# A state-space and expert layer: silu rebuilt from tanh tile by tile, its product on GpSimd, and four smaller edits

## The chip, the cores and the metric

One Trainium2 chip, one of its cores. A core has five engines that run their own instruction queues in order: TensorE (PE, matmuls and transposes into PSUM; PEld is its weight load), VectorE (DVE), ScalarE (ACT, activations), GpSimd (POOL, elementwise products here) and SyncE (SP, which issues the DMAs). The metric is the device time of the whole program in microseconds (us), the median of several runs. Less is better.

## The reference

The input u has 4 sequences of 2048 steps with 256 features. Two parts follow, each with a residual sum:

```
n      = layernorm(u)                                  # eps 1e-5, no affine part
x, z   = split(n @ W_in.T + b_in)                      # 512 inner channels each
dbc    = x @ W_x.T + b_x                               # 16 + 16 + 16 columns: raw delta, B, C
delta  = softplus(raw @ W_dt.T + b_dt);  A = -exp(A_log)
h      = h * exp(delta * A) + x * delta * B            # over time, 512 channels x 16 states
y      = sum_n(h * C) + x * D
u1     = u + (y * z * sigmoid(z)) @ W_out.T + b_out    # z * sigmoid(z) is silu
n      = layernorm(u1)
w      = the two largest of softmax(n @ Wg.T + bg) over 4 experts
h_e    = relu(n @ Wi.T + lowrank_e)                    # 1024 wide, rank 4 an expert
out    = u1 + sum_e w_e * (h_e @ Wo.T)
```

All numbers are float32.

## The kernel before

Time is cut into 16 chunks of 512 steps. Channels lie on the 128 partitions, so a chunk has four channel tiles (ND = 4) of 128 x 512, and each of them has 16 states: 64 scans of 128 x 512 a chunk, 1024 in all. "State i" below is the i-th of these scans.

The loop over the states (lines after `for i in range(M + 4)`) gives each state: `decay` (ACT, exp of delta times A into a PSUM tile dA of a pool of three banks, two states ahead), `enter` (POOL, the product dBx of x times delta with B for two states at once, four states ahead, three buffers), `scan` (DVE, one instruction over 512 steps, in place in PSUM, or into SBUF as hS for one state in four), `read` (the product with C: DVE's hC, or for that one in four POOL's hP), `keep` (ACT copies the last column as the carry) and `sum_y` (PE transposes the product and adds it up in the PSUM tile y). B and C come from DRAM by broadcast DMAs on SP, some groups of four states ahead.

Everything else is a list of steps that is filled in between the states: `front` (LayerNorm statistics on DVE, its reciprocal root on POOL in `rstd`, normalising on ACT, transposes, the projections `p_in`, `p_dbc`, `p_dt`, softplus over all four tiles in one activation), the gate (`p_in` for z, `a_in` with the bias, and `silu`, one activation over 128 x 2048), `tail` (out projection and residual), and `ffn` (routing, then the inner layer by half rows of 512). Front and gate run for the chunk to come, the inner layer lags by up to two chunks. A `Pacer` writes the order out by hand: it carries planned times for each engine, places a step where its own plan lets it start in time (BEGIN, END, MARGIN are its limits), counts three PSUM banks for all such steps (`takes`, `gives`), and forces steps that others are about to need (`force`: the silu before a chunk's y is closed, softplus and the delta-x products before the next chunk's first product). It plans one order for each engine; the chip then runs these orders.

In the inner layer, half row k (NK = 8 a chunk) takes one bank. Before the change `p_base` opens it with two matmuls by Wi, `p_low` adds the low-rank part of the second expert's slot, a first relu reads it, `p_low` of the next k adds the first slot's part, a second relu reads it, and `p_hT` transposes both relus together; `p_down` multiplies by Wo.

ACT holds one set of function tables at a time; a load stands before softplus and silu, and another before the exp that follows. In the first chunk the name `xdts` for the products of delta and x is taken over by the next chunk's, so the forcing at state 27, which is meant for chunk 0's last product, asks for chunk 1's.

Of the kernel before, what the change touches and what calls it, by code (L numbers as in the profile page):

```python
# [13 lines left out]
P = 128  # L14
# [30 lines left out]
class Pacer:  # L45
# [6 lines left out]

    BEGIN = {"pe": 0.7, "act": 0.6, "pool": 0.5, "sp": 0.0}
    END = {"pe": 2.2, "act": 1.5, "pool": 2.5, "sp": 99.0}
# [114 lines left out]
def ssm_moe_layer_kernel(  # L169
# [115 lines left out]
    nc.gpsimd.memset(lowm, 0.0)  # L285

    carry = const.tile([P, ND, N], F32, tag="carry", name="carry")

# [4 lines left out]
    pacer = Pacer(BANKS)  # L293
    st = {}

# [28 lines left out]
    def layernorm_T(src, dst, name, then=None):  # L324

        q = {}

        def stats(j):
            if j == 0:
                q["mv"] = small.tile([P, NJ, 2], F32, tag=f"mv{name[0]}", name=f"mv_{name}")  # L330
            x = small.tile([P, 6], F32, tag="st", name=f"st_{name}_{j}")
            dve.bn_stats(x, src()[:, j, :])
            dve.bn_aggr(q["mv"][:, j, :], x)

        def rstd():

            ve = small.tile([P, NJ], F32, tag="ve", name=f"ve_{name}")
# [25 lines left out]

        steps = [Step("dve", 0.54, lambda j=j: stats(j)) for j in range(NJ)]
        steps += [Step("pool", 1.95, rstd)]
# [26 lines left out]
    def front(c, norm, taken=()):  # L392
# [13 lines left out]
        def hold(k):  # L406
            if k not in s:
                s[k] = chunk.tile([P, ND, TC], F32, tag=k, name=f"{k}_{c}")
            return s[k]

        def a_in(dst, m, mw):
            act.activation(hold(dst)[:, m, :], q["in", mw], AF.Identity, bias=b_in_sb[:, mw : mw + 1])

# [37 lines left out]
        def xdt(m):  # L451
            pool.tensor_tensor(hold("xdt")[:, m, :], s["delta"][:, m, :], s["xT"][:, m, :], ALU.mult)

        def silu():
            act.activation(s["g"], s["g"], AF.Silu)

# [23 lines left out]
        for m in range(ND):  # L480
            gate.append(Step("pe", 1.75, lambda m=m: p_in(ND + m), after=[ln], takes=1))
            gate.append(Step("act", 0.57, lambda m=m: a_in("g", m, ND + m), gives=1))
        gate.append(Step("act", 4.4, silu))
        return steps, gate, dbc, xdts

    def open_y(c, d):
# [5 lines left out]
        def scale():  # L492
            q["xd"] = work.tile([P, TC], F32, tag="xd", name=f"xd_{c}_{d}", bufs=1)
            act.activation(q["xd"], s["xT"][:, d, :], AF.Copy, scale=d_sb[:, d : d + 1])

# [62 lines left out]
    def ffn(c):  # L558
# [102 lines left out]
        def p_base(k):  # L661
            j, half = divmod(k, 2)
            pm = q["z", k] = mm_tile(f"pz_{c}_{k}")
# [74 lines left out]
        z1s, hs, copies = [], [], []  # L738
        bases = [Step("pe", 1.75, lambda k=k: p_base(k), after=[last], takes=1) for k in range(NK)]
        steps.append(bases[0])  # L740
# [119 lines left out]
    def begin(c):  # L860
# [13 lines left out]
        if c + 1 < NCHUNK:  # L874
            norm = norms.pop(c + 1, None) or front_norm(c + 1)
            f, g, *deadline[c + 1] = front(c + 1, norm[NJ if c else 0 :], [g[-3]])
            g[0].after += gate_after
            silus[c + 1] = g[-1]
            if not c:
# [16 lines left out]
    act.activation(spare, mhalf[:, 0:1], AF.Softplus)  # L896
    f, g, dbc, xdts = front(0, front_norm(0))
    pacer.add(f)
    pacer.force(f[2 * NJ])
    join_x()  # L900
    pacer.force(dbc)
    silus[0] = g[-1]
# [5 lines left out]
    pacer.force(xdts[0])  # L908

# [3 lines left out]
    for i in range(0, AHEAD_B, NN):  # L913
        pacer.force(xdts[states[i][2]])
        X[i] = X[i + 1] = pacer.run("pool", 2.32, lambda: enter(i))
# [8 lines left out]
    for i in range(M + 4):  # L924
# [109 lines left out]
```

## Time and profile before

| what | value |
|---|---|
| median of 3 runs | 2129.7 us (2126.46 to 2132.01) |
| profiled execution | 2129.43 us, span 2127.7 us |
| granted TensorE clock, mean | 0.929 |
| busy: PE, DVE, POOL, ACT | 88%, 87%, 80%, 68% of the span |
| first scan starts, last scan ends | 31.6, 2014.8 us |
| scans on DVE | 1024, 1.21 to 1.28 us each |
| dBx products on POOL | 512, 2.363 us each |
| table loads on ACT | 64, 1.283 us each |

A group's row in the profile has the line, the engine, the operation, what it writes and reads, the count, then the busy time in us and the mean length of one in ns, then the idle time of the engine just before them and what ended most of it. A row in order of time has the start and the length in us, and in brackets the idle time before it and who ended it. A row of waits has who waited for whom, the sum in us, how often, and the longest. Instructions of one engine overlap by some 0.03 to 0.1 us, so a busy sum is a little over the time it fills, and where steps are added up the distance from start to start is used. All steps pass through one helper, so their line is L30, and groups are told apart by their tiles.

### The profile page before, as it was taken

Reading aid. Unit: us, or ns where it says so; the run is one execution under the profiler, and the core shown is the slowest. Engines: PE = TensorE matmul, PEld = TensorE weight load, DVE = VectorE, ACT = ScalarE, POOL = GpSimd, SP = SyncE. Lnnn points to the kernel's source line nnn. Section 1 sums busy time; section 2 is a strip of 40 time slices with the busy share of each in tenths; the row PEclk is TensorE's granted clock in tenths of the full one; section 3 lists DMA queues with packets and bytes.
Section 4 is the critical chain, followed back from the end, with each engine's and each line's share of the span. In section 5 each row is a group of like instructions: output and inputs, shape, how many; then the busy total and the mean of one; then the engine's idle time right before and its main releaser. Section 6 shows DMA issues by size and latency. Waiting matters only on the chain.

```text
span 2127.7 us, 28591 instructions
## 1 busy us (share of the span) xinstructions
PE 1873.9 (88%) x9504; PEld 1284.0 (60%) x9504; DVE 1855.8 (87%) x2423; ACT 1441.7 (68%) x2898; POOL 1709.4 (80%) x1084
## 2 busy tenths in 40 slices
PE   7768788998889989899899988989899998989978
PEld 4445555665566665657666565766657575666655
DVE  4899898999989989999989998999989999999810
ACT  5857667667676667676767777676677867766522
POOL 5898888989878878888888888888888888878600
PEclk9859799998999999999999999999999999989989
DMA  7454344445444443434435454444535444444200
GB/s 218 144 165 152 127 150 149 149 147 161 151 139 151 149 140 138 169 130 149 163 130 164 140 167 132 147 152 139 169 130 173 136 141 149 138 149 140 98 10 10
DMA packets 106132, 300.70 MB, mean 141 GB/s; under 512 B 12864, under 2 KB 39104, under 8 KB 105984
## 3 DMA queue, kind: packets, MB, share of 16 engines
q1 hardware_dynamic: 105984, 298.88, 42.8%
q8 instruction: 74, 1.21, 0.2%
q14 instruction: 74, 0.61, 0.1%
HBM read 289.41 MB, written 9.44 MB: 140 GB/s over the span
## 4 chain that ended last, share of the span: by engine, by line
PE 25%; DVE 20%; ACT 12%; issue 5%; POOL 1%; DVEq 0%; POOLq 0%; ACTq 0%
DVE dA L30 9%; PE pz L30 9%; PE y L30 5%; PE pf L30 5%; ACT dA L30 5%; DVE hC L30 4%; DVE hS L30 4%; PE phT L30 3%; ACT L30 2%; ACT h L30 1%; PE pin L30 1%; ACT delta L30 1%; ACT g L30 1%; DVE u L30 1%; DVE plg L30 1%
## 5 line engine op out<-in xcount | busy, mean ns | idle before, releaser
L30 POOL TENSOR_TENSOR dBx<-xdt,B 128x1024 f32<-128x1024 f32 x512 | 1207.8, 2363 | 187.5 <-DVE dA L30 157.3
L30 ACT ACTIVATE dA<-delta,a_sb 128x512 f32<-128x512 f32 x1024 | 706.8, 693 | 143.0 <-DVE hC L30 66.8
L30 DVE TENSOR_TENSOR_SCAN dA<-dA,carry,dBx 128x512 f32<-128x512 f32 x576 | 726.4, 1279 | 62.6 <-ACT dA L30 51.0
L30 PE MATMUL y<-ident,hC 128*128 128x128 f32 x3072 | 490.7, 291 | 36.6 <-DVE hC L30 36.5
L30 DVE TENSOR_TENSOR hC<-dA,C 128x512 f32<-128x512 f32 x768 | 514.1, 670 | 0.2 <-issue 0.2
L30 PEld LDWEIGHTS y<-ident,hC 128*128 128x128 f32 x3072 | 386.1, 150 | 181.3 <-issue 73.6
L30 POOL TENSOR_TENSOR hP<-hS,C 128x512 f32<-128x512 f32 x256 | 326.6, 1276 | 5.1 <-issue 4.1
L30 PE MATMUL pz<-wi_sb,x2T 128*128 128x512 f32 x512 | 271.7, 657 | 25.2 <-ACT hT L30 15.4
L30 DVE TENSOR_TENSOR_SCAN dA<-dA,dBx 128x512 f32<-128x512 f32 x192 | 231.2, 1220 | 35.3 <-ACT dA L30 30.5
L30 DVE TENSOR_TENSOR_SCAN hS<-dA,carry,dBx 128x512 f32<-128x512 f32 x192 | 244.1, 1271 | 18.6 <-ACT carry L30 10.6
L30 PE MATMUL pf<-wo_sb,hT 128*128 128x256 f32 x1024 | 243.4, 383 | 11.6 <-ACT hT L30 9.4
L30 PE MATMUL pin<-xnT,w_in_sb 128*128 128x512 f32 x512 | 245.9, 612 | 5.5 <-ACT g L30 3.6
L30 ACT COPY carry<-dA 128x1 f32<-128x1 f32 x576 | 90.1, 157 | 208.5 <-DVE hC L30 206.5
L30 ACT ACTIVATE h<-pz,topv 128x512 f32<-128x512 f32 x256 | 165.4, 680 | 74.1 <-PE pz L30 73.4
L30 PEld LDWEIGHTS pf<-wo_sb,hT 128*128 128x128 f32 x1024 | 186.5, 190 | 41.6 <-ACT hT L30 14.4
L30 PEld LDWEIGHTS y<-ident,hP 128*128 128x128 f32 x1024 | 128.3, 148 | 96.3 <-issue 56.7
L30 PE MATMUL y<-ident,hP 128*128 128x128 f32 x1024 | 167.1, 288 | 18.7 <-POOL hP L30 18.7
L30 PEld LDWEIGHTS pz<-wi_sb,x2T 128*128 128x128 f32 x512 | 95.2, 207 | 124.9 <-issue 76.2
L30 PE MATMUL pz<-bm_sb,lowT 16*128 16x512 f32 x512 | 167.9, 660 | 0.0
L30 PE MATMUL phT<-ident,h 128*128 128x128 f32 x1024 | 139.7, 281 | 21.3 <-ACT h L30 16.8
L30 PEld LDWEIGHTS pin<-xnT,w_in_sb 128*128 128x128 f32 x512 | 92.3, 197 | 93.1 <-issue 75.2
L30 PEld LDWEIGHTS phT<-ident,h 128*128 128x128 f32 x1024 | 120.8, 145 | 44.2 <-ACT h L30 19.5
(94 smaller groups left out, 1784.8 us busy)
## 6 DMA issues: line engine op xcount, KB each, us to landing
B<-bc SPq DMA_DIRECT2D x256, 512.0 KB, 3.7
C<-bc SPq DMA_DIRECT2D x256, 512.0 KB, 3.7
ua<-in_u_dram SPq DMA_DIRECT2D x16, 512.0 KB, 5.5
u<-in_u_dram SPq DMA_DIRECT2D x16, 512.0 KB, 4.4
out_dram<-u SPq DMA_DIRECT2D x16, 512.0 KB, 4.8
w_in_sb<-in_w_inT_dram SPq DMA_DIRECT2D x2, 512.0 KB, 4.7
wi_sb<-in_wiT_dram SPq DMA_DIRECT2D x1, 1024.0 KB, 6.7
wo_sb<-in_woT_dram SPq DMA_DIRECT2D x1, 1024.0 KB, 10.4
```

What stands on the lines that cost most here:

```text
L30: return self._tc.keep_in_program_order(f(*args, **kwargs))
```

## The change

Silu is computed as (1 + tanh(z/2)) * z/2. `a_half` writes z/2 in place of z (the bias halved once at the start in `bh_sb`, on POOL, and a scale of 0.5); `tanh` is two activations for each channel tile, tanh and the addition of 1, into a tile th with two buffers; `silu` is a product on POOL for each tile. The tile m waits for the product of two tiles before. Closing a y forces only its own tile's product.

The low-rank part of slot 1 opens the inner layer's bank (`start` moves from `p_base` to `p_low`), and `p_base` comes behind it; the bank is taken there, and the base of the next half row no longer starts ahead.

In LayerNorm the addition of eps and the sign of the mean go from POOL to DVE, as two operations on the four columns of mv behind the last statistics; POOL keeps the power and one product.

`first_xdts` keeps chunk 0's products apart, so the forcing at state 27 asks for these.

x is held in half-chunk tiles with three buffers, in place of one tile a chunk with two. The planner lets POOL's steps begin up to 1.0 in place of 0.5 ahead of DVE's plan, and its costs follow the new steps. The built program has 32 table loads in place of 64.

```
-    BEGIN = {"pe": 0.7, "act": 0.6, "pool": 0.5, "sp": 0.0}
+    BEGIN = {"pe": 0.7, "act": 0.6, "pool": 1.0, "sp": 0.0}
...
+    bh_sb = const.tile([P, ND], F32, tag="bh_sb", name="bh_sb")
+    nc.gpsimd.tensor_scalar_mul(bh_sb, b_in_sb[:, ND:], 0.5)
...
             dve.bn_aggr(q["mv"][:, j, :], x)
+            if j == NJ - 1:
+                q["nm"], q["ve"] = q["mv"][:, :, 0], q["mv"][:, :, 1]
+                dve.tensor_scalar_mul(q["nm"], q["nm"], -1.0)
+                dve.tensor_scalar(q["ve"], q["ve"], EPS, None, ALU.add)
...
-            pool.tensor_scalar_add(ve, q["mv"][:, :, 1], EPS)
-            pool.tensor_tensor(q["rstd"], ve, mhalf, ALU.pow)
-            pool.tensor_tensor(ve, q["mv"][:, :, 0], q["rstd"], ALU.mult)
-            pool.tensor_scalar_mul(q["nmr"], ve, -1.0)
+            pool.tensor_tensor(q["rstd"], q["ve"], mhalf, ALU.pow)
+            pool.tensor_tensor(q["nmr"], q["nm"], q["rstd"], ALU.mult)
...
+        def x_of(m):
+            k = "xT", m // ND2
+            if k not in s:
+                s[k] = chunk.tile([P, ND2, TC], F32, tag="xT", name=f"xT_{c}_{m // ND2}", bufs=3)
+            return s[k][:, m % ND2, :]
...
-        def silu():
-            act.activation(s["g"], s["g"], AF.Silu)
+        def a_half(m):
+            mw = ND + m
+            act.activation(hold("g")[:, m, :], q["in", mw], AF.Identity, bias=bh_sb[:, m : m + 1], scale=0.5)
+
+        def tanh(m):
+            q["th", m] = work.tile([P, TC], F32, tag="th", name=f"th_{c}_{m}")
+            act.activation(q["th", m], s["g"][:, m, :], AF.Tanh)
+            act.activation(q["th", m], q["th", m], AF.Copy, bias=1.0)
+
+        def silu(m):
+            g = s["g"][:, m, :]
+            pool.tensor_tensor(g, q["th", m], g, ALU.mult)
...
-            gate.append(Step("act", 0.57, lambda m=m: a_in("g", m, ND + m), gives=1))
-        gate.append(Step("act", 4.4, silu))
+            gate.append(Step("act", 0.57, lambda m=m: a_half(m), gives=1))
+            gate.append(Step("act", 1.02, lambda m=m: tanh(m)))
+            gate[-1].after = gate[-2:-1] + halves[-2:-1]
+            gate.append(Step("pool", 1.23, lambda m=m: silu(m)))
+            halves.append(gate[-1])
...
         def p_base(k):
-                    start=(m == 0), stop=False, skip_group_check=True,
+                    start=False, stop=True, skip_group_check=True,
...
         def p_low(k):
+                    if slot:
+                        q["z", x] = mm_tile(f"pz_{c}_{x}")
...
-                        rhs=bm_sb[r, half * HF : (half + 1) * HF], start=False, stop=True,
+                        rhs=bm_sb[r, half * HF : (half + 1) * HF], start=bool(slot), stop=not slot,
...
-                "pe", 1.06 if 0 < k < NK else 1.05, lambda k=k: p_low(k), after=bases[k : k + 1] + z1s[-1:]
+                "pe", 1.06 if 0 < k < NK else 1.05, lambda k=k: p_low(k), after=[last] + z1s[-1:], takes=int(k < NK)
...
-                z1s.append(Step("act", 0.57, lambda k=k: a_relu(k, 1), after=[low]))
-                steps.append(z1s[-1])
-            steps += bases[k + 1 : k + 2]
+                bases.append(Step("pe", 1.75, lambda k=k: p_base(k), after=[low]))
+                z1s.append(Step("act", 0.57, lambda k=k: a_relu(k, 1), after=bases[-1:]))
+                steps += [bases[-1], z1s[-1]]
...
-                pacer.force(silus[c])
-                steps[0].after = [pacer.run("act", 0.5, copy, [Y[i - 3]]), silus[c]]
+                pacer.force(silus[c][d])
+                steps[0].after = [pacer.run("act", 0.5, copy, [Y[i - 3]]), silus[c][d]]
...
             if i == PER // NH - AHEAD_B - 1:
-                pacer.force(xdts[-1])
+                pacer.force(first_xdts[-1])
```

More of the change, by code (lines that the diff above doesn't have):

```diff
@@ L293, in ssm_moe_layer_kernel @@
     pacer = Pacer(BANKS)
-    st = {}
+    st, halves = {}, []
     wc_sb = const.tile([P, KM, NX + R], F32, tag="wc_sb", name="wc_sb")
@@ L333, in stats @@
             dve.bn_aggr(q["mv"][:, j, :], x)
+            if j == NJ - 1:
+                q["nm"], q["ve"] = q["mv"][:, :, 0], q["mv"][:, :, 1]
+                dve.tensor_scalar_mul(q["nm"], q["nm"], -1.0)
+                dve.tensor_scalar(q["ve"], q["ve"], EPS, None, ALU.add)
         def rstd():
-            ve = small.tile([P, NJ], F32, tag="ve", name=f"ve_{name}")
             q["rstd"] = small.tile([P, NJ], F32, tag="rstd", name=f"rstd_{name}")
             q["nmr"] = small.tile([P, NJ], F32, tag="nmr", name=f"nmr_{name}")
-            pool.tensor_scalar_add(ve, q["mv"][:, :, 1], EPS)
-            pool.tensor_tensor(q["rstd"], ve, mhalf, ALU.pow)
-            pool.tensor_tensor(ve, q["mv"][:, :, 0], q["rstd"], ALU.mult)
-            pool.tensor_scalar_mul(q["nmr"], ve, -1.0)
+            pool.tensor_tensor(q["rstd"], q["ve"], mhalf, ALU.pow)
+            pool.tensor_tensor(q["nmr"], q["nm"], q["rstd"], ALU.mult)
         def norm(j):
@@ L364, in layernorm_T @@
         steps = [Step("dve", 0.54, lambda j=j: stats(j)) for j in range(NJ)]
-        steps += [Step("pool", 1.95, rstd)]
+        steps += [Step("pool", 1.35, rstd)]
         steps += [Step("act", 0.5, lambda j=j: norm(j), locks=j == 0) for j in range(NJ)]
@@ L409, in hold @@
             return s[k]
+        def x_of(m):
[3 more added lines that the diff above has]
+            return s[k][:, m % ND2, :]
+        s["x"] = x_of
         def a_in(dst, m, mw):
-            act.activation(hold(dst)[:, m, :], q["in", mw], AF.Identity, bias=b_in_sb[:, mw : mw + 1])
+            act.activation(x_of(m) if dst == "xT" else hold(dst)[:, m, :], q["in", mw], AF.Identity, bias=b_in_sb[:, mw : mw + 1])
         def p_dbc():
@@ L451, in xdt @@
         def xdt(m):
-            pool.tensor_tensor(hold("xdt")[:, m, :], s["delta"][:, m, :], s["xT"][:, m, :], ALU.mult)
-        def silu():
-            act.activation(s["g"], s["g"], AF.Silu)
+            pool.tensor_tensor(hold("xdt")[:, m, :], s["delta"][:, m, :], x_of(m), ALU.mult)
+        def a_half(m):
[8 more added lines that the diff above has]
+            pool.tensor_tensor(g, q["th", m], g, ALU.mult)
         steps = list(norm)
@@ L493, in scale @@
             q["xd"] = work.tile([P, TC], F32, tag="xd", name=f"xd_{c}_{d}", bufs=1)
-            act.activation(q["xd"], s["xT"][:, d, :], AF.Copy, scale=d_sb[:, d : d + 1])
+            act.activation(q["xd"], s["x"](d), AF.Copy, scale=d_sb[:, d : d + 1])
         def turn():
@@ L662, in p_base @@
             j, half = divmod(k, 2)
-            pm = q["z", k] = mm_tile(f"pz_{c}_{k}")
+            pm = q["z", k]
             for m in range(KM):
@@ L738, in ffn @@
         z1s, hs, copies = [], [], []
-        bases = [Step("pe", 1.75, lambda k=k: p_base(k), after=[last], takes=1) for k in range(NK)]
-        steps.append(bases[0])
+        bases = []
         for k in range(NK + 1):
             low = Step(
-                "pe", 1.06 if 0 < k < NK else 1.05, lambda k=k: p_low(k), after=bases[k : k + 1] + z1s[-1:]
+                "pe", 1.06 if 0 < k < NK else 1.05, lambda k=k: p_low(k), after=[last] + z1s[-1:], takes=int(k < NK)
             )
@@ L875, in begin @@
             norm = norms.pop(c + 1, None) or front_norm(c + 1)
-            f, g, *deadline[c + 1] = front(c + 1, norm[NJ if c else 0 :], [g[-3]])
+            f, g, *deadline[c + 1] = front(c + 1, norm[NJ if c else 0 :], [g[-4]])
             g[0].after += gate_after
-            silus[c + 1] = g[-1]
+            silus[c + 1] = g[3::4]
             if not c:
@@ L896, in ssm_moe_layer_kernel @@
     act.activation(spare, mhalf[:, 0:1], AF.Softplus)
-    f, g, dbc, xdts = front(0, front_norm(0))
+    f, g, dbc, first_xdts = front(0, front_norm(0))
     pacer.add(f)
@@ L901, in ssm_moe_layer_kernel @@
     pacer.force(dbc)
-    silus[0] = g[-1]
+    silus[0] = g[3::4]
     loaded = next(x for x in f if x.engine == "sp")
@@ L907, in ssm_moe_layer_kernel @@
         load_bc(i, 1)
-    pacer.force(xdts[0])
+    pacer.force(first_xdts[0])
     act.activation(a_sb, a_sb, AF.Exp)
@@ L913, in ssm_moe_layer_kernel @@
     for i in range(0, AHEAD_B, NN):
-        pacer.force(xdts[states[i][2]])
+        pacer.force(first_xdts[states[i][2]])
         X[i] = X[i + 1] = pacer.run("pool", 2.32, lambda: enter(i))
```

## The prediction

> **What bounds the kernel now.** I read the page first, then the stretches before and after the last scan, then the groups of VectorE and ScalarE, then the order of time around one silu and around the last chunk.
>
> ```profile
> span 2127.7 us, 28591 instructions
> PE 1873.9 (88%) x9504; PEld 1284.0 (60%) x9504; DVE 1855.8 (87%) x2423; ACT 1441.7 (68%) x2898; POOL 1709.4 (80%) x1084
> ```
>
> No engine is full over the whole span, so it has to be cut. The busy time by stretch (us of PE, PEld, DVE, ACT, POOL, then granted clock, DMA share, GB/s); the first scan starts at 31.6, the last ends at 2014.8:
>
> ```profile
> 31.60:2014.80 1983.20, 1759.39 (x9040) 1211.82 (x9040) 1839.58 (x2374) 1396.83 (x2824) 1699.75 (x1056) 0.93 0.45 148
> 2014.80:2071.90 57.10, 44.26 (x208) 31.91 (x206) 10.06 (x31) 14.27 (x27) 3.11 (x10) 0.86 0.03 10
> 2071.90:2127.70 55.80, 49.68 (x196) 28.45 (x196) 1.70 (x4) 15.51 (x25) 0.00 (x0) 0.96 0.03 10
> ```
>
> For 1983 us the 1024 scans run, and DVE is busy in 93% of it; its true idle time there, gap by gap, is 134 us, and 116 of them end with ACT. After that 113 us belong to PE. What ends DVE's idle time, and what the largest of it is:
>
> ```profile
> DVE dA L30 <- ACT dA L30: 81.5, 129, 6.1
> ...
> DVE hS L30 <- ACT carry L30: 21.0, 10, 6.5
> ...
> L30 ACT ACT_TABLE_LOAD x64 | 82.1, 1283 | 1.8 <-PEq L1021 0.7
> ...
> L30 ACT ACTIVATE g<-g 128x2048 f32<-128x2048 f32 x16 | 30.6, 1912 | 0.2
> ...
> 102.89 1.28 ACT L30 ACT_TABLE_LOAD   x1
> 104.19 1.91 ACT L30 ACTIVATE g<-g 128x2048 f32<-128x2048 f32 x1
> ...
> 106.16 1.28 ACT L30 ACT_TABLE_LOAD   x1
> 107.46 0.69 ACT L30 ACTIVATE dA<-delta,a_sb 128x512 f32<-128x512 f32 x1
> ...
> 108.18 2.35 DVE L30 TENSOR_TENSOR_SCAN dA<-dA,dBx 128x512 f32<-128x512 f32 x2 [2.20 <-ACT dA L30]
> ```
>
> The reader is to see one silu: load, 2048 columns, load back, and only then the decay that the next scan needs. Three dA banks let ACT run two states ahead, about 3.5 us of DVE work; 4.4 us between two decays overrun it by 2.2.
>
> **The change, part by part** (orders are those of the two built programs, durations are rows of this execution).
>
> Silu. 32 of 64 table loads and 16 long activations go. DVE's idle time before the scan behind each was 2.3, 2.2, 2.4, 2.8, 0, 1.4, 2.3, 1.6, 2.2, 1.8, 2.1, 1.6, 2.2, 1.8, 2.1, 2.1: 30.6 us. All of it goes: -30.6 (ends -31 and -25). ACT's own time hardly changes: 2 x 1.295 + 1.82 = 4.4 us a chunk from start to start against four times two activations of 128x512. Tanh is in no row; hT<-phT takes 585 ns and dA 693, so a dependent pair is 1.15 to 1.35, four are 4.6 to 5.4. The Trainium skill, "ScalarE: Activation LUTs", section What ACT_TABLE_LOAD costs, puts a switch at 1283 ns plus a drain of about 1380; by it 32 switches would free 85 us of ACT, by the row (next instruction 1.295 behind) 41. The trace decides, and ACT's total time isn't the bound.
>
> What comes in their place. Between two decays the new order has 61 places with 1.5 to 4 us of other ACT work, where the old has 27; 26 of these lay in the loop with whole rows, and none was followed by an idle DVE. Places with 0.25 to 1.25 us go from 598 to 622, and cost 0.1 each before (59.6 us in 598). So tanh costs 2.4 plus 34 x 0.15 = 7; ends 0 and 34 x 0.5 = 17 + 2.4. I take 7, near the rows that stalled nothing.
>
> Softplus. 15 stand in the loop and cost 23.9 us, 13 unforced ones 0.65 each, up to 2.3. In the new order 14 stand alone; 14 x 0.65 = 9, at the worst like the silus 14 x 2 = 28. The wrong delta: state 27 of chunk 0 forced chunk 1's last delta x, which put its softplus at state 29 with 6.15 us of ACT work and an idle time of 6.07. Now chunk 1's front is held until its own deadline: LayerNorm, transposes and dbc (3.52 us of ACT) at state 52, xT, four deltas and softplus (7.88) at 56. The rows are 6.07 for 6.15 and 6.45 for 6.73; I take 9 for both, 6 to 14. Together 18 against 23.9: -6 (-9 to +18). With it the two bc writes of 32 KB and the next ua load move on SP's queue from behind the B loads of states 16 to 20 to those of state 48; write and B load land in 3.2 + 3.7 us, the first product that reads them is issued at state 60, 8 x 1.9 us on, so they stay covered. If they were late, the first scan of chunk 1 would wait by the difference.
>
> LayerNorm. POOL loses two small operations in each of 32 (228 and 242 ns), DVE gains two. On DVE the last aggregation is now waited for: 0.21 where the next started 0.10 behind, and two operations at 0.09 (m's step): 0.3 x 31 in the loop = +9 (6 if only the steps count, 12 if the first costs its full 0.18). DVE is the engine in want there, so it is charged in full; in the tail POOL's shorter chain pays it back.
>
> POOL gets 64 products at the rate of xdt, 1.225 from start to start: 4.9 us a chunk, less 1.2 for LayerNorm. A chunk's POOL work goes from 106.4 to some 110 us of 124. dBx waits for DVE 157 us in all today, so there is room; bursts of eight states reach 19 us where 18.2 passed without a stall. +3 (0 to 8). What is queued behind a product on POOL is dBx, four states ahead; DVE's gate multiply, which now waits for it, stands at least six states later. A tanh waits for the product two tiles before; if POOL were late, a decay behind it on ACT would be late with it, and a PSUM bank held.
>
> The half bias. The new product stands ahead of the first rstd on POOL and waits for b_in_sb, issued at 8.33, landing 1.8 later; rstd started at 7.47. The normalised tiles come 2.5 us later, but the transposes waited for PE until 12.7 anyway: +0.5.
>
> Banks. With the low-rank part first, PE's sequence per half row is low, base, phT; relu 1 (0.68) is covered by phT (0.96). In steady state nothing changes. What changes is how far the inner layer has come when the scans end:
>
> ```profile
> 2053.63 0.69 DVE L30 TENSOR_TENSOR u<-u,po 128x512 f32<-128x512 f32 x1 [2.71 <-PE po L30]
> ...
> 2059.19 2.80 PE L30 MATMUL pt_f<-ident,xn_f 128*128 128x128 f32 x8 [5.59 <-ACT xn_f L30]
> ...
> 2071.89 1.06 PE L30 MATMUL plT<-ident,lowm 128*64 128x128 f32 x4 [6.05 <-POOL lowm L30]
> ...
> 2086.22 1.04 PE L30 MATMUL phT<-ident,h 128*128 128x128 f32 x8
> ```
>
> Behind the last y the old order holds 3 base pairs of chunk 14, 9 low, 40 phT and 24 pf matmuls up to plT; the new one 7, 13, 64 and 32. That is 4 x 1.82 + 4 x 0.53 + 3 x 0.96 + 3.65 + one wait of 0.68 = 16.6 us more PE work after the scans. But the two chains in which PE stood idle (5.59 and 6.05) now have 4 us and 3.5 us of chunk 14 beside them: -7.5 to -8. Net +8 (5 to 12).
>
> The sum: -30.6 + 7 - 6 + 9 + 3 + 0.5 + 8 = -9. The profiled execution took 2129.43 (span 2127.7), like the median of 2129.7; I predict 2120. All good ends together give -28, all bad ones +45.
>
> **Where a row fails.** The two new DVE operations read and write SBUF with one source. No row shows such a multiply or add beside a POOL product: the one on a_sb ran while POOL was idle.
>
> ```profile
> L30 DVE RECIPROCAL sm<-sm 128x4 f32<-128x4 f32 x16 | 2.9, 178 | 0.6
> ...
> L30 DVE TENSOR_SCALAR a_sb<-a_sb 128x64 f32<-128x64 f32 x1 | 0.2, 195 | 15.0 <-ACT a_sb L30 15.0
> ```
>
> The nearest is the reciprocal, SBUF to SBUF, four columns: 10 of 16 ran beside a POOL product, all started 0.035 behind their forerunner and took 177 to 179 ns. So the sum has no wait. The far end: each waits for the product in flight. The Trainium skill, "SBUF — State Buffer", section Who interferes with whom, says that a one-source multiply between SBUF operands may use two ports and then is locked out for the whole of a GpSimd instruction; the reciprocal isn't in its list.
>
> **The rivals.**
>
> 1. DVE waits for POOL (slower). At the end of the last aggregation POOL was inside an instruction in 20 of 32 cases, with 0.6 us left on the mean of all. If the first operation waits: 31 x 0.6 = 19. If the second then waits for the next product, 20 x 1.3 to 2.4 = 26 to 47 more. On -9 that is +10 to +57: 2139 to 2186, and 2152 if the second waits 1.3 in half of the 20. It decides as soon as the mean wait of a LayerNorm is over 0.5 us. For it: POOL is busy in 86% of the loop. Against: the reciprocals.
>
> 2. The stalls are only cut in pieces (same). Each of 64 tanh pairs overruns its place by 0.3 us: 19 in place of 7, softplus right after the scans' y tiles close costs 1.2 in place of 0.65 (+8). Sum +11: 2131. For it: 14 softplus now stand where the silus stood. Against: places of 1.5 to 2 us that stalled nothing.
>
> 3. The inner layer isn't later on chip than before, since PE catches up in DVE's new idle time; then the +8 goes and it ends at 2112. Against: the order is fixed, and PE has 11% idle at a clock of 0.93.
>
> **How the numbers follow.** The forecast has 0.50 with its own range 2105 to 2135, rival 1 has 0.25, rival 2 0.18, rival 3 0.07. This kernel's runs tell 0.3% (6.4 us) from nothing: faster is under 2123, slower over 2136. Of the forecast 0.36 lies under, 0.12 between, 0.02 over; rival 3 is faster; rival 2 gives 0.13 same, 0.03 faster, 0.02 slower; rival 1 gives 0.23 slower and 0.02 same. Faster 0.46, same 0.27, slower 0.27. 2100 takes in all good ends; 2165 leaves out the upper half of rival 1's second wait: 2100 to 2165.
>
> **What would show it.** 32 table loads; the scans end some 17 us earlier, at 1997, and the part behind them is 8 longer. No stall over 1 us stands outside softplus. The new operation on mv_a takes some 0.1 to 0.2 us and starts at once; a mean wait of 0.5 us or more, with POOL in front, is rival 1. If DVE's idle time ended by ACT isn't near 86 us, the silu term failed; if POOL ends more than 15, the POOL term.

## The result and the profile after

| | before | after |
|---|---|---|
| median of 20 runs each | 2130.45 us (2126.46 to 2132.31) | 2134.02 us (2118.42 to 2144.47) |
| ratio after / before, 95% interval | | 1.0016 (0.9999 to 1.0033) |
| span of the profiled execution | 2127.7 | 2137.4 |
| first scan starts, last scan ends | 31.6, 2014.8 | 32.2, 2019.1 |
| from the last scan to the end | 112.9 | 118.3 |
| DVE idle between first and last scan, summed over gaps of more than 0.06 us | 133.7 | 106.7 |

No difference that can be measured: 2120 was forecast, 14 us less than the median. The profiled execution of after took 2139.22, 5 above its median, so its span overstates the change by that much. The head of the page of after:

```profile
span 2137.4 us, 28813 instructions
PE 1897.9 (89%) x9504; PEld 1301.8 (61%) x9504; DVE 1886.1 (88%) x2487; ACT 1448.1 (68%) x2978; POOL 1767.7 (83%) x1085
```

DVE is busy for 30.3 us more (1855.8 before) and has 64 more instructions. The same cut by stretch (us, busy time of PE, PEld, DVE, ACT, POOL, granted clock, DMA share, GB/s) shows where:

```profile
32.20:2019.10 1986.90, 1766.79 (x8974) 1221.28 (x8973) 1869.54 (x2434) 1395.60 (x2894) 1758.87 (x1060) 0.91 0.44 147
2019.10:2077.00 57.90, 56.53 (x258) 37.14 (x257) 7.45 (x20) 20.03 (x33) 1.22 (x2) 0.96 0.00 1
2077.00:2137.40 60.40, 52.78 (x212) 31.12 (x211) 4.50 (x18) 17.36 (x30) 1.40 (x6) 0.96 0.05 18
```

In the first stretch DVE's busy time rose by 29.9 (1839.58 before) while its idle time fell by 27.0: what the rest of the change gave there was spent, and the loop is 3.7 longer. Behind the scans PE is busy in 109.3 of 118.3 us, where it was busy in 93.9 of 112.9. DVE's longest waits and the groups of instructions that the change added:

```profile
DVE dA L30 <- ACT dA L30: 59.1, 125, 3.0
...
DVE hS L30 <- ACT carry L30: 16.9, 4, 9.9
```

```profile
L30 ACT ACT_TABLE_LOAD x32 | 41.1, 1283 | 1.3 <-PEq L1051 0.7
L30 ACT ACTIVATE th<-th 128x512 f32<-128x512 f32 x64 | 40.4, 631 | 2.0
L30 ACT ACTIVATE th<-g 128x512 f32<-128x512 f32 x64 | 39.8, 622 | 1.0
...
L30 DVE TENSOR_SCALAR mv_a<-mv_a 128x4 f32<-128x4 f32 x32 | 27.5, 902 | 0.6
L30 DVE TENSOR_SCALAR mv_f<-mv_f 128x4 f32<-128x4 f32 x32 | 4.7, 191 | 0.6
```

The wait for the decay is down from 81.5 to 59.1. The last two rows are the two small operations of LayerNorm: 902 ns on the mean for four columns in the LayerNorm of u (mv_a), 191 in the one of u1 (mv_f). The view of the one tile gives least, median and longest:

```profile
L30 DVE TENSOR_SCALAR mv_a<-mv_a x32: 155/602/4362, 6.9 to 1705.4; 128x4 f32<-128x4 f32 x32
```

And this is the longest of them in order of time:

```profile
1699.46 2.49 POOL L30 TENSOR_TENSOR xdt<-delta,xT 128x512 f32<-128x512 f32 x2
...
1700.92 0.18 DVE L30 BATCH_NORM_AGGREGATE mv_a<-st_a 128x2 f32<-128x6 f32 x1
1701.14 4.43 DVE L30 TENSOR_SCALAR mv_a<-mv_a 128x4 f32<-128x4 f32 x2
...
1701.91 2.35 POOL L30 TENSOR_TENSOR dBx<-xdt,B 128x1024 f32<-128x1024 f32 x1
...
1704.21 1.26 POOL L30 TENSOR_TENSOR xdt<-delta,xT 128x512 f32<-128x512 f32 x1
1705.48 1.27 DVE L30 TENSOR_TENSOR_SCAN hS<-dA,carry,dBx 128x512 f32<-128x512 f32 x1
```

The multiply starts at 1701.14, inside a product on POOL, and ends at 1705.50, when POOL's third product in a row ends at 1705.47. No semaphore is waited for: the wait lies inside the instruction, so the profile counts it as busy time, and a list of waits doesn't show it. The others are of the same kind: 19 of the 64 took over 0.22 us, and each of them started inside a POOL instruction and ended 24 to 32 ns behind the end of one. For 14 it was the product in flight. Four, each the second of its pair, started in the last 0.06 us of the product that the first had waited for, and waited for the whole of the next; the one shown waited through three. Without waits the 64 operations would take some 0.16 each (155 to 171 ns in the other 45), 10 us; they take 32.2 as the rows count them, and 35.0 summed one by one, since a row counts the overlap of a pair once. So some 25 us of DVE's time are waits for POOL.

### The profile page after: what moved, and what is told of

It is laid out like the page before. It is cut to its first block, busy times and chain, and to the rows that moved or that the text cites. A ratio compares the mean times of both kernels' runs of the same rounds, so it can differ in the third digit from the quotient of the medians.

```text
span 2137.4 us, 28813 instructions
## 1 busy us (share of the span) xinstructions
PE 1897.9 (89%) x9504; PEld 1301.8 (61%) x9504; DVE 1886.1 (88%) x2487; ACT 1448.1 (68%) x2978; POOL 1767.7 (83%) x1085
## 5 line engine op out<-in xcount | busy, mean ns | idle before, releaser
L30 PE MATMUL y<-ident,hC 128*128 128x128 f32 x3072 | 501.0, 296 | 39.7 <-DVE hC L30 39.4
L30 PEld LDWEIGHTS y<-ident,hC 128*128 128x128 f32 x3072 | 395.7, 153 | 187.7 <-issue 72.0
L30 PE MATMUL pz<-wi_sb,x2T 128*128 128x512 f32 x512 | 263.2, 639 | 0.0
L30 ACT ACTIVATE h<-pz,topv 128x512 f32<-128x512 f32 x256 | 173.3, 680 | 132.3 <-PE pz L30 131.5
L30 DVE TENSOR_TENSOR_SCAN dA<-dA,dBx 128x512 f32<-128x512 f32 x192 | 231.7, 1220 | 20.5 <-ACT dA L30 14.9
L30 PE MATMUL y<-ident,hP 128*128 128x128 f32 x1024 | 174.3, 297 | 50.0 <-POOL hP L30 50.0
L30 PE MATMUL pz<-bm_sb,lowT 16*128 16x512 f32 x512 | 175.0, 670 | 26.6 <-ACT delta L30 8.3
L30 PEld LDWEIGHTS pz<-wi_sb,x2T 128*128 128x128 f32 x512 | 93.7, 204 | 102.1 <-issue 102.1
L30 PE MATMUL phT<-ident,h 128*128 128x128 f32 x1024 | 135.3, 275 | 7.9 <-ACT h L30 7.0
```

Of the source, the lines that this page charges most:

```text
L30: return self._tc.keep_in_program_order(f(*args, **kwargs))
```

## Experiments: the LayerNorm operations

The kernel before was run beside each of these, at medians of 2129.6 to 2131.1, and the ratios are to those runs.

Theory 1: the multiplies are locked out by POOL's instructions, and this is what ate silu's gain. Rivals: the waits are taken up by idle time elsewhere, or the gain of silu was never there.

**The same operations as reductions.** Everything else of after stays, the orders of PE, ACT, POOL and SP too but for four fills of constants at the start. eps is added by summing the variance and a third column that holds it.

```
-                dve.tensor_scalar_mul(q["nm"], q["nm"], -1.0)
-                dve.tensor_scalar(q["ve"], q["ve"], EPS, None, ALU.add)
+                dve.tensor_reduce(q["nm"], q["mv"][:, :, 0:1], AX.X, ALU.add, negate=True)
+                dve.tensor_reduce(q["ve"], q["mv"][:, :, 1:3], AX.X, ALU.add)
```

> The changed kernel with LayerNorm's two small DVE operations written as reductions (the sign by a reduction over one column with negation, eps by a sum over the variance and a third column that holds eps); every engine's order stays. Theory lock (an SBUF-to-SBUF multiply or add on DVE waits for the POOL product in flight): the two groups on DVE fall from 32.2 us to about 5.5, no single one is over 0.25 us, and some 20 to 27 us of the span go: 2107 to 2114, and the spread of its runs shrinks. Theory dispatch (DVE loses the time to the wait for the last aggregation and to having two more operations, whatever their kind): the time stays at 2134 within 5.

Measured: 2102.31 (2100.02 to 2104.57), ratio to before 0.9868 (0.9855 to 0.9881), 31.7 us under after. The groups of this run:

```profile
L30 DVE TENSOR_REDUCE nm_a<-mva 128x4 f32<-128x4 f32 x16 | 2.5, 157 | 0.6
...
L30 DVE TENSOR_REDUCE ve_a<-mva 128x4 f32<-128x8 f32 x16 | 2.4, 151 | 0.0
```

37 of the 64 reductions ran within a POOL instruction, none took over 159 ns. The scans end at 1980.2 (after 2019.1), the part behind them is 118.0 (118.3). The time is some 5 under theory lock's range: by the two profiles DVE's busy time in the loop fell by 26.1, as the theory has it, and its idle time by 13.0 as well. Why the idle time fell isn't shown. The Trainium skill, "SBUF — State Buffer", section Who interferes with whom, says that a reduction has no two-port mode on this chip and so never contends with GpSimd: these rows agree. The rows of mv_a agree with what the same section says of a `tensor_scalar`, that it can enter the two-port modes and then contends.

**The LayerNorm part undone.** eps and sign go back to POOL as four small operations, DVE loses its two; the orders of PE, ACT and SP are those of after.

```
-                dve.tensor_scalar_mul(q["nm"], q["nm"], -1.0)
-                dve.tensor_scalar(q["ve"], q["ve"], EPS, None, ALU.add)
...
+            pool.tensor_scalar_add(ve, q["mv"][:, :, 1], EPS)
+            pool.tensor_tensor(q["rstd"], ve, mhalf, ALU.pow)
+            pool.tensor_tensor(ve, q["mv"][:, :, 0], q["rstd"], ALU.mult)
+            pool.tensor_scalar_mul(q["nmr"], ve, -1.0)
```

> The kernel after with its LayerNorm part alone undone: eps and sign go back to POOL, DVE loses the two operations; the orders of PE, ACT and SP are the ones of after. Theory 1 (the two DVE multiplies are locked out by POOL's products, and this costs the whole program its full length): what after spends on them is 32.2 us, and POOL gets 0.47 us back in each of 32 LayerNorms at 90% busy, so 2134 - 32 + (0 to 8) = 2102 to 2110, and the scans end some 25 us earlier than after's 2019.1. Rival (the waits are taken up by idle time elsewhere, as in the kernel before plus the LayerNorm part alone, and what made the reductions faster was another thing): 2125 to 2137, the scans end at 2010 to 2020, and DVE's idle time in the loop grows from 106.7 to 125 or more.

Measured: 2105.70 (2105.24 to 2107.47), ratio 0.9883 (0.9871 to 0.9896): theory 1. Its stretch of scans:

```profile
32.20:1986.20 1954.00, 1743.97 (x8976) 1210.75 (x8977) 1837.67 (x2374) 1396.27 (x2895) 1773.10 (x1120) 0.92 0.45 150
```

The row begins at after's 32.2; by its own first scan, at 32.0, the loop is 32.7 us shorter than after's. DVE's busy time is 31.9 lower, and its idle time is the same, 106.7. In this order the waits and the operations' own time cost their full length. With the two operations on DVE as reductions the kernel is 3.4 us faster than with them on POOL (2102.31 against 2105.70); the intervals overlap.

**The operations doubled.** Two more multiplies, by 1.0, behind the two.

```
                 dve.tensor_scalar(q["ve"], q["ve"], EPS, None, ALU.add)
+                dve.tensor_scalar_mul(q["nm"], q["nm"], 1.0)
+                dve.tensor_scalar_mul(q["ve"], q["ve"], 1.0)
```

> The kernel after with two further multiplies by 1.0 in each LayerNorm, on the same columns and straight behind the two that are there: 64 more operations on DVE, the result unchanged, all orders else as in after. Theory 1 (a LayerNorm pays for the lock once: the first operation waits for the product in flight, and behind it POOL is mostly idle, because its next operation waits for these): 64 x 0.1 to 0.17, 6 to 11 us more, 2140 to 2145. Theory 2 (each operation waits for itself, at the mean of 0.5 us that the 64 of after took): 32 us more, 2166, and to 2190 if POOL's products get in between.

Measured: 2151.19 (2147.77 to 2155.48), 17.2 more, between the two:

```profile
L30 DVE TENSOR_SCALAR mv_a<-mv_a 128x4 f32<-128x4 f32 x64 | 52.6, 877 | 0.6
L30 DVE TENSOR_SCALAR mv_f<-mv_f 128x4 f32<-128x4 f32 x64 | 8.4, 186 | 0.6
```

The mean of one hardly changes (902 to 877, 191 to 186), so the second pair pays about as much as the first: by place in the row of four they took 22.0, 14.1, 24.6 and 7.3 us in all. The scans ended 17.7 later while these rows grew by 28.8, since DVE's idle time fell from 106.7 to 97.3.

**The LayerNorm part alone on the kernel before**, once with multiplies as in the change, once with reductions. The first has before's orders on PE, ACT and SP:

```
-            pool.tensor_scalar_add(ve, q["mv"][:, :, 1], EPS)
-            pool.tensor_tensor(q["rstd"], ve, mhalf, ALU.pow)
-            pool.tensor_tensor(ve, q["mv"][:, :, 0], q["rstd"], ALU.mult)
-            pool.tensor_scalar_mul(q["nmr"], ve, -1.0)
+            pool.tensor_tensor(q["rstd"], q["ve"], mhalf, ALU.pow)
+            pool.tensor_tensor(q["nmr"], q["nm"], q["rstd"], ALU.mult)
```

> The kernel before with the LayerNorm part of the change alone; the order of PE, ACT and SP is that of before, and POOL has two small operations less in each of 32. Theory lock: the new DVE operations take 20 to 35 us in all, single ones 2 to 4 us, and the time is 15 to 25 us over before: 2145 to 2155. Theory dispatch: 64 operations at 0.1 and a wait of 0.1 each: 6 to 9 us over before, 2136 to 2139.

> The kernel before with the LayerNorm part alone, its two DVE operations written as reductions, which in the changed kernel took 151 to 157 ns each. With multiplies the same edit gave 2127.3, and the multiplies took 26.4 us of DVE there. Theory 1 (the lock costs its full length wherever DVE is in want): 26.4 - 9.8 = 16.6 us less, 2111, the range 2108 to 2116. Theory 2 (in the order of before, idle time behind ACT took up most of the waits, 133.7 us of it fell to 106.1): a third of that comes back, 2120 to 2126, and DVE's idle time in the loop returns to 118 to 130.

Measured: with multiplies, against both expectations of a loss, 2127.33 (2123.07 to 2133.18), ratio 0.9987 (0.9977 to 0.9998), though they took 26.4 us:

```profile
L30 DVE TENSOR_SCALAR mv_a<-mv_a 128x4 f32<-128x4 f32 x32 | 20.5, 684 | 0.6
L30 DVE TENSOR_SCALAR mv_f<-mv_f 128x4 f32<-128x4 f32 x32 | 5.9, 229 | 0.6
```

With reductions 2121.86 (2119.07 to 2123.85), ratio 0.9960 (0.9948 to 0.9973): 5.5 us less, where the operations became 16.6 us shorter. So the lock is there too, but in before's order two thirds of it vanish in idle time: DVE's fell from 133.7 to 106.1 with multiplies and stands at 116.1 with reductions. Theory 2 of the second expectation holds in its time; the idle time is a little under its 118. And without the lock the move to DVE is no loss: with reductions it is 0.4% faster than before. That the cover is the time behind silus and decays, in which ACT catches up while DVE waits for POOL, is read from which gaps shrank (the wait of dA for ACT went from 81.5 to 66.9 and back to 72.6), not tested by itself.

## Experiments: silu, the banks and the part behind the scans

**The silu part alone** on the kernel before (tanh, the product on POOL, x in half chunks; the lines are those of the change's diff), and **the bank part alone**, and **both**. The core of the second is

```
-        bases = [Step("pe", 1.75, lambda k=k: p_base(k), after=[last], takes=1) for k in range(NK)]
-        steps.append(bases[0])
+        bases = []
...
+                bases.append(Step("pe", 1.75, lambda k=k: p_base(k), after=[low]))
+                z1s.append(Step("act", 0.57, lambda k=k: a_relu(k, 1), after=bases[-1:]))
```

> The kernel before with silu by tanh, its product on POOL and x in half chunks, and nothing else. The prediction's terms: 30.6 us of stalls go, 7 come back, 3 for POOL. Its order has 118 us of PE matmul work behind the last y where before has 86 (at the steps of the last chunk of before), so the part behind the scans grows by 32 less what fills the two chains, 12 at most. Theory that the silu part pays its gain back behind the scans: scans end 15 to 25 us earlier than 2015, the rest is 20 to 30 longer, time 2125 to 2140. Theory that the tanh pairs stall the scans anew: scans end at 2005 or later and the time is over 2140.

> The kernel before with the low-rank part opening the inner layer's banks and nothing else. Behind the last y its order has 77 us of PE work where before has 86; the silus and softplus stay. Theory banks (a bank that is held for a shorter time lets the inner layer run further ahead): the part behind the scans is 6 to 10 us shorter, the scans end where they did, 2120 to 2124. Theory that the chain low, base, relu, low is longer and stalls ACT and through it the scans: no gain or a loss, 2130 to 2140.

> The kernel before with the silu part (2153.6 alone) and the low-rank part first in the banks (2134.7 alone) together. PE work in the built order behind the last y: 118.0 us with silu alone, 99.3 with both. Theory (the banks shorten the part behind the scans by what they move ahead of the last y, as 9.5 us of order gave 10.5 us on the chip): the rest goes from 143.5 to 123 to 126. In the loop the banks alone cost 15 us through relus that wait for PE ahead of decays on ACT (143.9 us of such waits against 73.4): if that is their nature, 2153.6 - 19 + 15 = 2150; if it was that order alone, 2135. A relu wait sum near 144 with the scans ending over 2022 is the first, near 131 with 2010 to 2015 the second.

| kernel | median | ratio (95%) | scans end | the rest (last scan to end) | PE work behind the last y in the built order | relus waiting for PE |
|---|---|---|---|---|---|---|
| before | 2130.45 | | 2014.8 | 112.9 | 86.2 | 73.4 |
| silu alone | 2153.62 | 1.0105 (1.0090 to 1.0121) | 2010.6 | 143.5 | 118.0 | 80.5 |
| banks alone | 2134.73 | 1.0020 (1.0012 to 1.0029) | 2029.8 | 102.4 | 76.7 | 143.9 |
| silu and banks | 2138.29 | 1.0032 (1.0018 to 1.0047) | 2016.3 | 124.6 | 99.3 | 133.3 |
| after | 2134.02 | 1.0016 (0.9999 to 1.0033) | 2019.1 | 118.3 | 102.1 | 131.5 |

(The sixth column counts matmuls of each kind by the time that each takes from start to start in before.) Against the expectations: silu alone has the longer rest of its first theory, but its time (over 2140) and its scans' end (after 2005) are those of the second, in which the tanh pairs stall the scans. Tanh pairs aren't what is seen, though. The longest of DVE's waits, the last number of this row, is 25.3 us in chunk 0,

```profile
DVE dA L30 <- ACT dA L30: 91.7, 133, 25.3
```

where the old forcing at state 27, which these kernels keep, puts all of chunk 1's front between two decays. Chunk 0 idles 30.9 us there, 13.2 before (small gaps counted). Banks alone fall in the second theory's 2130 to 2140. Both together lie between the two times named, with the rest (124.6) as expected and the relu waits and the scans' end near the second.

Three things follow. The rest goes with the lag of the inner layer that the planner builds: silu alone makes it 31.8 us of work and 30.6 us of time longer, and the banks take back 18.7 of work and 18.9 of time. So on the kernel before it is under the silu part that the planner lets the inner layer fall back, and the banks pull it forward, where the prediction had put the whole lag under the banks.

Second, the banks aren't free in the loop: alone they let the scans end 15.0 us later. The waits of ACT's relus for PE, before and with the banks alone:

```profile
ACT h L30 <- PE pz L30: 73.4, 67, 4.9
```

```profile
ACT h L30 <- PE pz L30: 143.9, 122, 5.9
```

One of them in order of time (banks alone), with DVE's scan behind it:

```profile
380.14 3.78 PE L30 MATMUL pz<-wi_sb,x2T 128*128 128x512 f32 x4
...
384.02 0.69 ACT L30 ACTIVATE h<-pz,topv 128x512 f32<-128x512 f32 x1 [3.60 <-PE pz L30]
...
384.65 0.70 ACT L30 ACTIVATE dA<-delta,a_sb 128x512 f32<-128x512 f32 x1
...
385.44 1.29 DVE L30 TENSOR_TENSOR_SCAN dA<-dA,carry,dBx 128x512 f32<-128x512 f32 x1 [2.96 <-issue]
```

The relu waits for its bank's base matmuls, which no longer start a half row ahead; the decay queued behind it on ACT is late, and the scan with it. Beside silu the same waits cost less: 133.3 us of them, but the scans end only 5.7 us later than with silu alone.

Third, silu and banks by themselves gain nothing in the loop: DVE's idle time is 132.5 with both, 133.7 before. The kernel without the LayerNorm part (2105.70) differs from this one (2138.29) only in `first_xdts`, in POOL's earlier begin (1.0 in place of 0.5) and in the planner's cost of a LayerNorm's POOL step (1.35 in place of 1.95), and is 32.6 us faster. The old forcing alone is worth 13.0 of it, as measured below beside reductions. By difference some 20 us hang on the planner's two numbers, which no run changes by themselves. The prediction prices the order that they helped to make, but has no term for them.

**The bank part undone in after**, with reductions in place of the locked multiplies; the base matmuls open the bank again:

```
+        bases = [Step("pe", 1.75, lambda k=k: p_base(k), after=[last], takes=1) for k in range(NK)]
+        steps.append(bases[0])
```

> The kernel after with the two LayerNorm operations as reductions (2102.3 alone), and the bank part undone: the base matmuls open the bank again, one half row ahead. In the built order 88.0 us of PE work stand behind the last y, 102.1 with the bank part. Theory 1 (the built order's lag sets the part behind the scans, and in this kernel the bank part makes it longer; it also makes relus wait for PE ahead of decays): the rest goes from 118 to 104, ACT's relu waits for PE from 118.5 to some 75 us, the loop is 0 to 15 us shorter, 2073 to 2088. Theory 2 (the bank part shortens what stands behind the scans, as it did by 10.5 us alone and by 19 us beside the silu part): the rest grows by 10 to 19, 2112 to 2121.

Measured: 2110.14 (2098.99 to 2113.88), ratio 0.9901 (0.9880 to 0.9922), 7.8 more than with the banks (2102.31); the intervals just touch. The relu waits fell to 67.7 and the rest to 111.7 (profiled at 2102.49), which is theory 1 for both, though the rest by 6 in place of 14. So in this order it is the bank part that makes the lag: 14.1 of the 15.9 us of PE work by which after's order exceeds before's. But the time missed theory 1's 2073 to 2088: the loop became 9.3 longer (1957.2 against 1947.9), where 0 to 15 less was expected. The planner makes another order when a bank is held longer, and some chunks stall more: chunk 4 lost 14.9 us in idle time in place of 4.8, chunk 0 22.5 in place of 19.1 (here and below small gaps are counted too). So the single price of the bank part has no fixed sign: it cost 4 us on before, gave 15 beside silu and 8 here, and costs 19 in the pair of kernels at the end of the next part. It depends on the order that the planner makes around it.

## Experiments: the first chunk

In after, chunk 0 has two stalls, the two largest of the loop, where the front of chunk 1 is held until its deadlines at states 52 and 56. The second in the rows of ACT and of DVE:

```profile
133.13 0.69 ACT L30 ACTIVATE xT<-pin,b_in_sb 128x512 f32<-128x512 f32 x1 [0.80 <-PE pin L30]
135.28 0.69 ACT L30 ACTIVATE xT<-pin,b_in_sb 128x512 f32<-128x512 f32 x1 [1.47 <-PE pin L30]
136.33 2.59 ACT L30 ACTIVATE delta<-pdt,b_dt_sb 128x512 f32<-128x512 f32 x4 [0.36 <-PE pdt L30]
138.94 1.28 ACT L30 ACT_TABLE_LOAD   x1
140.23 1.91 ACT L30 ACTIVATE delta<-delta 128x2048 f32<-128x2048 f32 x1
...
144.29 1.22 DVE L30 TENSOR_TENSOR_SCAN hS<-dA,dBx 128x512 f32<-128x512 f32 x1 [9.88 <-ACT carry L30]
```

ACT not only has 7.88 us of work in a row here, it also waits inside the burst for PE's projections, 2.6 us in the three rows shown. The first stall, of 5.46, has 2.50 of such a wait.

**The old forcing put back** (with reductions), and **the front forced in pieces** (with reductions; and the same with the bank part undone):

```
-                pacer.force(first_xdts[-1])
+                pacer.force(xdts[-1])
```

```
+            early = {24: 9, 30: 13, 36: 17, 40: 21, 44: 23, 46: 26}
+            if i in early:
+                pacer.force(soon[early[i]])        # soon: the steps of chunk 1's front
```

> The kernel after with the two operations as reductions (2102.3 alone), and the forcing at state 27 of chunk 0 put back to the other chunk's products. Theory (the held front's second burst, 5.46 + 9.88 us of idle in chunk 0, is dearer than the old force's 6.07): 9 us less, 2093. Rival (the old force in the new planner puts all of the next chunk's front, 12.55 us of ACT work, between two decays of state 29, as it did with the silu part alone, where chunk 0 lost 30.9 us): 12 to 16 us more, 2114 to 2118, with one idle time of 9 to 13 us near 90 us.

> The kernel after with the two LayerNorm operations as reductions (2102.3 alone), and chunk 1's front forced in six pieces at states 24 to 46 of chunk 0, in place of all at states 52 and 56; no other edit. The bursts of 3.52 and 7.88 us of ACT work between two decays are gone from the built order, softplus stands alone with 4.41 at state 48. Theory (the two stalls of 5.51 and 9.88 us in chunk 0 are the price of the bursts): chunk 0's large stalls fall to 2 to 4 us, and the PE work behind the last y goes from 102.1 to 95.5 us: 10 to 18 us less, 2084 to 2092. Rival (chunk 0 has no room on ACT or PE, and the work stalls the scans wherever it is put): 2098 to 2104.

> The two edits before together (reductions, early pieces of chunk 1's front, bank part undone); 88.0 us of PE work behind the last y. If both theories hold and their gains add, 2102.3 - (10 to 14) - (14 to 29): 2060 to 2078, with the rest near 104. If the bank part's undoing lengthens the rest, 2100 or more.

Measured: the old forcing 2115.26 (2111.64 to 2116.52), 13.0 more than 2102.31, the rival in its time. In the new order it puts the whole front between two decays, and one gap holds it all, twice as long as the rival's 9 to 13:

```profile
106.47 1.23 DVE L30 TENSOR_TENSOR_SCAN dA<-dA,dBx 128x512 f32<-128x512 f32 x1 [21.35 <-ACT dA L30]
```

The pieces: 2116.12 (2114.85 to 2120.79), 13.8 more, a miss for both expectations. Chunk 0 did what was expected: 118.8 us in place of 125.4, idle 11.7 in place of 19.1. But chunks 4, 5, 6 and 13 lost 43.0 us in idle time in place of 21.0, and the rest grew to 120.9, although its work in the order is 6.6 less. With the steps forced early at the start, the planned order of the chunks behind is another one as well.

With the bank part undone as well: 2097.14 (2095.43 to 2098.18), ratio 0.9849 (0.9836 to 0.9862), 13.0 less than the same kernel without the pieces (2110.14) and 19.0 less than with the pieces and the bank part (2116.12). There chunk 0 went from 128.9 to 116.8. By the two profiles the chunks behind it took 6.9 of these 12.1 us back, but the profiled run without the pieces (2102.49) was 7.7 under its median. It missed its expectation of 2060 to 2078, which had added up gains of which only one was real, but it is the fastest kernel of the study, 1.5% under before; the one with reductions alone, at 0.9868 (0.9855 to 0.9881), can't be told from it by the intervals.

## Why the prediction was wrong

The failed step is the LayerNorm term. The prediction put it at +9, wrote "So the sum has no wait", and took the reciprocal as the nearest row. Measured on after it is 28.3 us (2134.02 less 2105.70 without the part, which also gives POOL its two operations back) or 32.7 in the loops of the two profiles. What it charged for, the wait for the last aggregation and two more steps on DVE, isn't seen as a loss: as reductions, which have both, the two operations left the kernel 3.4 us faster than with them on POOL. The price is that of the multiplies' waits for POOL, some 25 us by the trace, which it put at nothing. The reciprocal is another operation: its rows beside POOL's products were true and said nothing of a multiply. The rule of the Trainium skill, "SBUF — State Buffer", section Who interferes with whom, which the prediction set against this, was right, and the trace of before had no row of the kind that could speak for or against it. Rival 1 is what happened: the waits average 0.78 us a LayerNorm (25 us in 32), over the 0.5 from which it was to decide. Its price, 45 to 66 with the second wait, was too high, as the second operation took 13.0 us in all, 4 of 32 over 0.3 us.

The other terms:

- Silu, its places and softplus: -30.6 + 7 - 6, with +3 for POOL and 0.5 at the start: a loop shorter by 26.6 without LayerNorm. DVE's idle time fell by 27.0. That is true of the order as built, not of silu: silu and banks alone took 1.2 us off it, and the rest came with the order that `first_xdts` and the planner's two numbers made. The prediction counted its places in this order and put the gain down to silu. Inside the sum two errors partly cancel. Chunk 0's held front costs 15.3, where "I take 9 for both, 6 to 14" stood: it counted ACT's work and not ACT's waits for PE inside the burst. The places of tanh cost less than the 7: DVE's gaps that a decay ended with no table load near rose from 47.7 to 52.8. The other softplus cost 8.8 for 9.
- DVE's idle time ended by ACT is 86.9, 86 was predicted; tanh and its addition take 622 and 631 ns, a pair 1.25; 32 loads. POOL ends 2.4 us of DVE's idle time in the loop, so the term of 3 for POOL stands where waits are seen; what POOL really cost doesn't show as a wait.
- "No stall over 1 us stands outside softplus" failed: there are eighteen of 1.0 to 5.5, among them two residual sums that wait for PE (8.3 us) and the first stall of chunk 0. They cost no more than predicted in sum.
- The part behind the scans: +16.6 of PE work less 7.5 to 8, net +8. PE's busy time there rose by 15.4, its idle time fell by 10.0: +5.4. Right in its mechanism and, in this order, in its heading: without the banks 14.1 us of the work and 6.3 of the rest go. On the kernel before it is silu that builds the lag, and the banks reduce it.
- "In steady state nothing changes" of the banks was wrong. The relus' waits for PE went from 73.4 to 131.5; with the banks alone they went to 143.9, and the scans ended 15 us later. In after the bank part costs nothing that is seen, and by the runs its sign depends on the order around it.
- The start: +0.6 for +0.5.
- Two sums of the prediction don't come out. 4.4 us between two decays are 0.9 over the 3.5 that it allows, not 2.2; the 2.2 is the idle time in its row. And rival 2's "Sum +11" is over the time before, so it means 2141, not 2131, and its chance belonged to slower.

Without the LayerNorm term the prediction's sum is -18; the kernel without that part is 24.8 under before (2105.70 against 2130.45). So the forecast of a gain was true of the rest of the change, though not of silu and the banks by themselves, and one term of 9 that measured 28 to 33 took all of it. The stated range, 2100 to 2165, held the time.

## What to carry to other kernels

Before a one-source operation on SBUF operands moves to VectorE beside a busy GpSimd, look for a row of that very kind of operation; another four-column operation that never waits proves nothing, and the lock shows as a long instruction, not as a wait. A reduction can do the same arithmetic without it: here 157 ns in place of a mean of 902. Where an order is planned, an edit moves everything behind it: undo one part at a time on the finished kernel and on the first one, since the LayerNorm part cost nothing on the one and 28 us in the other.

## What the runs showed that was not expected

- A multiply on four columns took up to 4.36 us: it waited through three POOL products in a row. A wait isn't always over with the product in flight: for one of the 19 long ones, POOL's next two products went first.
- In the order of before, 19 us of such waits (29.2 summed one by one, less 10) on an engine that is busy in 93% of the loop left the time at 0.9987; in the order of after, 25 us of them and the operations' own time cost their full length.
- After's runs spread over 26 us (2118.42 to 2144.47), before's over 6; with reductions the spread is 4.6, without the LayerNorm part 2.2. Whether the chance meetings of multiplies and products make the spread was not tested; silu with banks on before, which has no such multiply, spreads over 18, and the kernel with reductions and the bank part undone over 15.
- The granted TensorE clock goes with the bank part: on the mean of its runs it is 0.911 to 0.923 in each of the eight kernels that have it, and 0.927 to 0.937 in each of the six that don't. Among after's own runs the slower ones have the lower clock (2118.42 us at 0.923, 2144.47 at 0.911). Which is the cause isn't shown. It isn't the whole of what the LayerNorm runs show: after's three runs at 0.922 or more took 2118.4 to 2124.3, and the slowest without the LayerNorm part 2107.47 at 0.917.
